# Late blocks' query features from unstacked pairs, in quarters of the PE array's rows, in one run with a chunk's sums

## The chip, the cores and the metric

The kernel runs on one core of one Trainium2 chip. The metric is the device time of one execution in microseconds (us), and a measured time is the median of several executions. The core has a matrix engine (TensorE, "PE" in the profile, with its weight loads listed apart as "PEld"), three engines that work on elements (VectorE "DVE", ScalarE "ACT", GpSimd "POOL"), and a queue engine (SyncE "SP") that here only issues transfers (DMAs). Every engine works through its own list of instructions in order and waits on semaphores for the others. PE reads operands from the on-chip memory SBUF and writes its results to PSUM, eight banks of 128 partitions x 512 float32.

## What is computed

One decoder layer on `x` of shape (2, 2048, 512): linear attention with 16 heads, then cross attention to 154 context rows, then a mixture of experts, each on a layer norm and added to `x`. The change lies in the linear attention alone:

```
q_proj = _elu1(jnp.einsum('bhnd,hdf->bhnf', q, proj_matrix))     # 32 -> 128 features a head
k_proj = _elu1(jnp.einsum('bhnd,hdf->bhnf', k, proj_matrix))
kv = jnp.einsum('bhnf,bhnd->bhfd', k_proj, v)
attn = jnp.einsum('bhnf,bhfd->bhnd', q_proj, kv)
k_sum = k_proj.sum(axis=2)
z = 1.0 / (jnp.einsum('bhnf,bhf->bhn', q_proj, k_sum) + 1e-08)
```

`_elu1(x)` is `x + 1` above zero and `exp(x)` below. Every head has 32 dimensions, so the product that makes its features contracts over 32 rows only.

## The kernel before

The 4096 tokens are eight blocks of 512 (`nblk` = 8, `TB` = 512); four blocks make one batch (`bpb` = 4). Blocks 0 to 3 are called early here, blocks 4 to 7 late. A block's 512 channels are four chunks of 128, and a chunk is four heads. Products that must keep float32 accuracy are made of pairs: a value is split into a high part in the fast format `float32r` and a low part, and three products (high x high, low x high, high x low; the list `TERMS`) are summed in PSUM.

The work on PE is of two kinds. *Dense* work is a queue of generators (`Dense`), each yielding after one matmul; `dense.fill(n)` issues n of them, and `dense.after(n, f)` calls f after n further ones. *Column* work (`columns.matmul`, L229) is pinned to program order with `tc.keep_in_program_order`; the rest may be moved by the scheduler of the tile framework, which writes the final list of each engine from its own timeline. So the order that runs is not the order of the source.

Query features, before. Each chunk of queries lies in DRAM as a pair `qd[b][c]` (high, low; 128 rows x 512 tokens). `load_queries` (L472) reads it with `stack` (L292) in three transfers of 256 KB (high, low, high) into a tile `qst` of 96 partitions: for each head the three parts stand below one another. The projection weights stand likewise stacked in `pst` (high, high, low). One matmul of 96 rows a head (`query_features`, L476, PE line L479, PSUM tile `pqp`) then makes the sum of the three terms at once. `features` (L361) follows: `relu(-x)` on ACT (L364), `exp(-.)` on ACT (L365), and `max(x, 0) + e` on DVE (L366), which is the last reader of the PSUM bank. The banks of `pqp` come from the pool `sc`, which has four.

A chunk's sums: `numerators` (L485, tile `pn`) and `denominators` (L507, tile `pd`) are eight float32 matmuls with 32 columns each, four heads side by side in the array's column quarters, all at L230. Float32 takes two passes, so the trace shows 16 instructions for a chunk.

`attended` (L558) multiplies numerators and reciprocals: POOL (L563, needs the transfers `num<-numd` for early blocks and `zr<-zd`), then ACT (L564), then DVE (L118); the result feeds the output projection `attention_outs` (dense, tile `po_a`, with a load `xr_a`, a POOL add L312 and a DVE add L315).

The late loop (L1346 to L1385) is where the change lies. Its step n handles late chunk n of 16: it loads the next chunk's queries, makes chunk n's features (two heads in each half of the step), fills in 26 (later 28) dense matmuls, calls `attended` for one half block according to the table `ahead` (L1345), and ends with the sums of chunk n - 1. Ahead of it the loop at L1334 ends the keys of the last block; behind it the cross attention begins, whose scores (`psc`) use the same four banks of `sc`.

Of the kernel before, what the change touches and what calls it, by code (L numbers as in the profile page):

```python
# [9 lines left out]
F32 = mybir.dt.float32  # L10
FR = mybir.dt.float32r
# [6 lines left out]
P = 128  # L18
D = 512
NC = D // P  # L20
H = 16
HD = 32
FEAT = 128
TB = 512
# [13 lines left out]
def decoder_layer(  # L38
# [26 lines left out]
    nc = tc.nc  # L65
    tokens = x.shape[0]
    nblk = tokens // TB
    bpb = nblk // batches
# [7 lines left out]
    sc = ctx.enter_context(tc.tile_pool(name="sc", bufs=SC, space=PSUM))  # L76
    dram = ctx.enter_context(tc.tile_pool(name="dram", bufs=1, space=DRAM))
    summed_up = ctx.enter_context(ExitStack())
    rows = ctx.enter_context(ExitStack())
# [18 lines left out]
    def eight(shape, dtype, name):  # L98
        return big.tile(shape, dtype, tag="b8", name=name)

    def half(name, dtype=F32):
        return work.tile([P, 512], dtype, tag="kp", name=name, bufs=9)
# [13 lines left out]
    def low(dst, src, hi, eng=None):  # L116

        (eng or nc.vector).tensor_tensor(dst, src, hi.bitcast(F32), ALU.subtract)  # L118

    def load_weight(w, name):  # L120
        raw = eight([P, NC, w.shape[1]], F32, f"raw_{name}")
        for k in range(NC):
            nc.sync.dma_start(out=raw[:, k], in_=w[k * P : (k + 1) * P, :])
        return [raw[:, k] for k in range(NC)]

    def split_weight(raw, name, busy=False):

        hi = eight([P, NC, D], FR, f"{name}_hi")
        lo = eight([P, NC, D], FR, f"{name}_lo")
        for k in range(NC):  # L130
            if isinstance(raw, list):
                part = raw[k]
            else:
                part = load_tile(raw, 0, k, name)
            if busy:
                nc.gpsimd.tensor_scalar(hi[:, k], part, 1.0, None, ALU.mult)
            else:
                nc.scalar.copy(hi[:, k], part)
            low(lo[:, k], part, hi[:, k], nc.gpsimd if busy or k % 2 else nc.vector)
        return hi, lo  # L140

    TERMS = ((0, 0), (1, 0), (0, 1))
# [90 lines left out]
    columns = Columns()  # L233
# [97 lines left out]
    raw = wk  # L331
    wk = [eight([P, NC, D], FR, f"wk_{i}") for i in ("hi", "lo")]
    for t in range(NT):
# [5 lines left out]
        b = nc.vector.tensor_tensor(lo, pt, hi.bitcast(F32), ALU.subtract)  # L339
        c = nc.scalar.copy(wk[0][:, t], raw[t])  # L340
        d = (nc.gpsimd if t % 2 else nc.vector).tensor_tensor(wk[1][:, t], raw[t], wk[0][:, t].bitcast(F32), ALU.subtract)
# [6 lines left out]
    rest = slice(2 * HD, 3 * HD)  # L348
    low(pst[rest], praw[rest], pst[rest])
    wq = split_weight(load_weight(w_qkv[:, :D], "wq"), "wq")  # L350

    kvs, kszs, pkvs, kaccs, made_kv = [], [], [], [], []
    qd = [[dram.tile([2, P, TB], F32, name=f"qd{b}_{c}") for c in range(NC)] for b in range(nblk)]
# [7 lines left out]
    def features(src, name, e=None):  # L361

        e = half(f"e_{name}") if e is None else e
        nc.scalar.activation(e, src, AF.Relu, scale=-1.0)  # L364
        nc.scalar.activation(e, e, AF.Exp, scale=-1.0)  # L365
        nc.vector.scalar_tensor_tensor(e, src, 0.0, e, ALU.max, ALU.add)  # L366
        return e
# [101 lines left out]

    qsts, qps, pds, nums, numd, zrs, zds, ats = {}, {}, {}, {}, {}, {}, {}, {}  # L470

    def load_queries(b, c):  # L472
        qsts[b, c] = eight([3 * HD, 4, TB], FR, f"qst{b}_{c}")
        stack(qsts[b, c], qd[b][c])

    def query_features(b, c, h):  # L476
        head = slice((4 * c + h) * FEAT, (4 * c + h + 1) * FEAT)
        pp = sc.tile([P, TB], F32, tag="sc", name=f"pqp{b}_{c}_{h}")
        nc.tensor.matmul(pp, lhsT=pst[:, head], rhs=qsts[b, c][:, h, :], start=True, stop=True)  # L479
        e = None  # L480
        if b < bpb and h:
            e = early.tile([P, TB], F32, tag="eq", name=f"eq{b}_{c}_{h}")
        qps[b, c, h] = features(pp, f"q{b}_{c}_{h}", e)

    def numerators(b, c):  # L485
        if c == 0:
# [20 lines left out]
    def denominators(b, c):  # L507
        if c == 0:
            pds[b] = bank(f"pd{b}")
        for h in range(4):  # L510
            columns.matmul(
                pds[b][h * HD : (h + 1) * HD, :],
                lhsT=kszs[b // bpb][:, c, h, :],
                rhs=qps.pop((b, c, h)),
                start=c == 0,
                stop=c == NC - 1,
                skip_group_check=True,
            )
        if c == NC - 1:
            reciprocals(b, pds.pop(b))  # L520
# [23 lines left out]
    def load_numerators(b):  # L544
        nums[b] = eight([P, NC, TB], F32, f"num{b}")
        nc.gpsimd.dma_start(out=nums[b], in_=numd[b])
# [220 lines left out]
    for s in range(ws_gate.shape[1] // F):  # L767
# [9 lines left out]
        out=before,  # L777
        in_=before,
# [503 lines left out]
    chunks = [(b, c) for b in range(nblk) for c in range(NC)]  # L1282
    shift = 2
    per = NC * NT
# [21 lines left out]
    for n in range(nblk * per):  # L1306
        b, c, t = n // per, n // NT % NC, n % NT
        dense.fill(58 if n == 0 else fl(n, 9.25) if n < 32 else fl(n, 9.5))
        if (b, c, t) == (nblk - 1, 0, 0):
            context_load()  # L1310
        if (b, c, t) == (nblk - 1, 1, 0):
            xwk = split_weight(wk_t, "xwk")
            dense.add(*(context_key(i, xwk) for i in range(NC)))
        if (b, c, t) == (nblk - 1, 2, 0):
            xwv = split_weight(wv_t, "xwv")
            bvr = half("bvr")
            nc.sync.dma_start(out=bvr, in_=bv.to_broadcast([P, D]))
            for bt in range(batches):
                dense.add(*(context_value(bt, at, xwv, bvr) for at in range(0, keys, P)))
        if (b, c, t) == (nblk - 1, 3, 0):  # L1320
            load_numerators(0)
            load_reciprocals(0, 0)
            bout = load_row(b_out, "bout")
        dense.until(stks, (b, c))
        key_features(b, c, t)
        todo.append((b, c, t))
        m = n - bpb * per - shift
        if m == -4:
            load_queries(0, 0)
        if m >= 0:  # L1330
            query_step(m)
        if n % 2 and len(todo) > LAG:
            sums_step(m)
    for m in range((nblk - bpb) * per - shift, (nblk - bpb) * per + NT):  # L1334
        dense.fill(5)
        query_step(m)
        if m % 2:
            sums_step(m)
        if m % 4 == 1:
            load_queries(*chunks[bpb * NC])  # L1340

    wout = split_weight(w_out, "wout")
    steps = chunks[bpb * NC :]

    ahead = {n if n < 13 else n + 2: ((n - 1) // 2, (n - 1) % 2 * 2) for n in range(1, 15)}  # L1345
    for n in range(len(steps) + 1):  # L1346
        if n < len(steps):
            b, c = steps[n]
            if n + 1 < len(steps):
                load_queries(*steps[n + 1])  # L1350
        if n + 1 in ahead:
            load_reciprocals(*ahead[n + 1])
        if n == 7:
            ln, tr = layernorm(x1[0], 0, 0, qts, "x")
            dense.add(*ln[:3])
            ln = ln[3:]
        if n == 8:
            dense.add(*tr[:1], *ln, *tr[1:])
        if n == 11:
            dense.add(*(cross_query(0, i) for i in range(NC)))  # L1360
        for i in range(2):
            if n < len(steps):
                query_features(b, c, 2 * i)
                query_features(b, c, 2 * i + 1)
            dense.fill(fl(2 * n + i, 13 if n < 12 else 14))
            if n in ahead:
                attended(ahead[n][0], ahead[n][1] + i)
                if ahead[n][1] and i:
                    whole = ahead[n][0]
                    if whole < nblk - 2:  # L1370
                        dense.add(*attention_outs(whole))
                    if whole + 1 < bpb:
                        load_numerators(whole + 1)
            if n and i:
                columns.batch()
                numerators(*steps[n - 1])
                denominators(*steps[n - 1])
        if n == 10:
            xwq = split_weight(wq_t, "xwq")
        if n == 11:  # L1380
            open_early.clear()
            attending.close()
            res = attending.enter_context(tc.tile_pool(name="res", bufs=1))
            for i in range(NC):
                load_keys(0, i)  # L1385
# [3 lines left out]
    steps = [(b, c, t) for b in range(nblk) for c in range(NC) for t in range(NT)]  # L1389
    for n in range(len(steps) + LAG + 1):  # L1390
        if n < len(steps):
            b, c, t = steps[n]
# [44 lines left out]
        if n > LAG:  # L1437
            b, c, t = steps[n - LAG - 1]
# [47 lines left out]
    for n, (group, u) in enumerate(todo3):  # L1486
# [3 lines left out]
        ahead = [[], []]  # L1490
        if u == len(units) - 2 and more:
            ahead = [expert_ahead(b) for b in range(group[-1] + 1, group[-1] + 3)]
# [8 lines left out]
        if n == LAST:  # L1501
            f0, f1 = finished(g, 0), finished(g, 1)
            d = downs
# [115 lines left out]
```

## Time and profile before

| | |
|---|---|
| median of 3 executions | 2331.12 us (2327.53 to 2331.25) |
| the profiled execution | 2329.48 us, of which the span is 2327.8 us |
| granted PE clock over the span | 0.982 of full speed |
| PE / DVE / ACT / POOL busy | 96% / 72% / 47% / 53% |
| late loop, first to last `pn` and `pd` of late blocks | about 494 to 648 us of the span |
| 486 to 648 us: PE busy, DMA share | 149.59 of 162 us, 0.94 at 260 GB/s |
| stacked query loads `qst<-qd` | 96 transfers of 256 KB in all, 48 of them for late blocks |

How to read it: the span is the time between the first and the last instruction that the profiler saw, and the execution's own time is 1.7 us longer. A matmul's listed duration covers its passage through a pipeline, so matmuls that follow one another overlap and their pace is read from the distance of two starts. A number in brackets behind an instruction is the engine's idle time ahead of it, with what ended it. The DMA share is the mean busy share of 16 DMA engines; values around 1 mean that transfers queue.

### The profile page before, as it was taken

To read this page: it belongs to the slowest core of one execution; us is meant where nothing else is said; L and a number is where in the kernel's file an instruction comes from. 1 tells how busy PE (TensorE), PEld (TensorE's weight loads), DVE (VectorE), ACT (ScalarE), POOL (GpSimd) and SP (SyncE) were. 2 spreads that over 40 slices of the span, in tenths; PEclk is the share of its full clock that TensorE was granted. 3 is DMA by queue.
4 is the path that set the end of the run, shared out by engine and by line. 5 is a ranking of instruction groups with operands and counts; after the bars stand their busy time and mean duration, and the time that the engine had idled before them with its cause. 6 is when DMAs were issued, how large, how long until landed. Compare 5 with 4: busy or idle time off the path is not lost.

```text
span 2327.8 us, 35169 instructions
## 1 busy us (share of the span) xinstructions
PE 2243.1 (96%) x11978; PEld 1740.2 (75%) x11978; DVE 1677.8 (72%) x2733; ACT 1102.0 (47%) x2598; POOL 1224.0 (53%) x1078
## 2 busy tenths in 40 slices
PE   7999999898999999999999999999989999999998
PEld 5888777645667777766788777888878888788887
DVE  6554555568687777778877777787797877877776
ACT  4555776756566777765343343222433223332221
POOL 5545433546475565654765553555484554755543
PEclk9999999999999999999999999999999999999999
DMA  6556777899975566565866657665557656575553
GB/s 211 178 170 179 203 217 217 241 256 268 261 215 149 166 186 167 175 195 212 291 237 228 234 192 295 225 229 217 181 197 293 242 211 231 178 280 208 205 192 129
DMA packets 201809, 498.23 MB, mean 214 GB/s; under 512 B 27738, under 2 KB 47578, under 8 KB 181694
## 3 DMA queue, kind: packets, MB, share of 16 engines
q1 hardware_dynamic: 199902, 489.89, 64.2%
q0 software_dynamic: 1728, 6.09, 0.9%
q8 instruction: 96, 1.57, 0.3%
q14 instruction: 83, 0.68, 0.1%
HBM read 351.30 MB, written 144.60 MB: 213 GB/s over the span
## 4 chain that ended last, share of the span: by engine, by line
PE 73%; DMA 12%; DVE 7%; issue 3%; POOL 2%; ACT 2%; SPq 1%; DVEq 0%; ACTq 0%; POOLq 0%
PE pg L1082 29%; PE pf L1195 11%; PE pf L148 4%; PE pk L148 3%; PE pq L148 3%; PE pv L148 3%; PE po_x L148 3%; PE xpq L148 2%; PE pp L402 2%; PE pc L745 2%; DMA qst<-qd 2%; PE psc L693 2%; PE pkv L230 1%; PE xpt L725 1%; PE po_a L148 1%
## 5 line engine op out<-in xcount | busy, mean ns | idle before, releaser
L1082 PE MATMUL pg<-xo,wq 128*128 128x512 f32 x3360 | 825.2, 392 | 2.5 <-DMA wq<-wqs 1.3
L1082 PEld LDWEIGHTS pg<-xo,wq 128*128 128x128 f32 x3360 | 630.5, 188 | 142.4 <-ACT s L1093 2.0
L1216 DVE TENSOR_TENSOR sum<-sum,pf 128x512 f32<-128x512 f32 x376 | 251.0, 683 | 50.5 <-PE pf L1195 43.9
L407 POOL TENSOR_TENSOR kacc<-kacc,e_k 128x512 f32<-128x512 f32 x128 | 166.1, 1298 | 224.1 <-DVE e_k L366 211.0
L703 ACT ACTIVATE xe<-psc,nb 128x154 f32<-128x154 f32 x512 | 195.2, 414 | 88.2 <-DVE nb L700 84.1
L708 POOL TENSOR_TENSOR xe<-xe,sm 128x616 f32<-128x616 f32 x128 | 157.6, 1237 | 94.5 <-DVE sm L707 73.2
L1195 PE MATMUL pf<-ht,wdo 128*128 128x512 f32 x696 | 188.4, 395 | 10.9 <-DVE sum L1216 10.9
L1145 POOL TENSOR_TENSOR u<-u,gr 128x512 f32<-128x512 f32 x48 | 65.7, 1368 | 238.8 <-DVE u L1114 237.4
L366 DVE SCALAR_TENSOR_TENSOR e_k<-pp,e_k 128x512 f32<-128x512 f32 x128 | 87.4, 685 | 107.5 <-ACT e_k L365 101.7
L1195 PEld LDWEIGHTS pf<-ht,wdo 128*128 128x128 f32 x696 | 130.9, 189 | 41.4 <-DVE sum L1216 12.0
L1195 PE MATMUL pf<-hb,wdo 128*128 128x512 f32 x522 | 148.2, 399 | 0.0
L1113 ACT ACTIVATE u<-u 128x512 f32<-128x512 f32 x80 | 50.6, 633 | 203.1 <-DVE u L1102 202.9
L148 PE MATMUL pf<-wd,hp 128*128 128x512 f32 x528 | 134.9, 403 | 4.7 <-DVE mv_n L248 3.4
L148 PEld LDWEIGHTS pf<-wd,hp 128*128 128x128 f32 x528 | 100.4, 192 | 33.2 <-issue 6.3
L700 DVE TENSOR_REDUCE nb<-psc 128x2 f32<-128x308 f32 x256 | 111.7, 466 | 11.9 <-PE psc L693 11.8
L703 ACT ACTIVATION_READ_ACCUMULATOR xe<-psc,nb 128x1 f32 x512 | 117.2, 229 | 0.0
L1102 DVE TENSOR_TENSOR u<-u,pg 128x512 f32<-128x512 f32 x160 | 108.5, 682 | 10.8 <-PE pg L1082 9.6
L1195 PEld LDWEIGHTS pf<-hb,wdo 128*128 128x128 f32 x522 | 98.1, 189 | 22.4 <-DVE sum L1216 0.8
L364 ACT ACTIVATE e_k<-pp 128x512 f32<-128x512 f32 x128 | 76.8, 601 | 69.7 <-PE pp L402 61.8
L693 PE MATMUL psc<-xkst,xst 96*128 96x154 f32 x512 | 93.8, 291 | 9.2 <-ACT xe L703 8.7
L693 PEld LDWEIGHTS psc<-xkst,xst 96*128 96x128 f32 x512 | 79.7, 197 | 25.2 <-ACT xe L703 16.1
L402 PEld LDWEIGHTS pp<-pst,kst 96*128 96x128 f32 x512 | 75.8, 191 | 26.7 <-issue 8.1
(285 smaller groups left out, 5137.6 us busy)
## 6 DMA issues: line engine op xcount, KB each, us to landing
wq<-wqs SPq DMA_DIRECT2D x90, 1024.0 KB
wqs<-wq SPq DMA_DIRECT2D x30, 1024.0 KB
wdo<-wds SPq DMA_DIRECT2D x29, 1024.0 KB
kst<-kd SPq DMA_DIRECT2D x96, 256.0 KB
qst<-qd SPq DMA_DIRECT2D x96, 256.0 KB
xst<-xqd SPq DMA_DIRECT2D x96, 256.0 KB
wdo<-wds SPq DMA_DIRECT2D x29, 768.0 KB
kd<-khl SPq DMA_DIRECT2D x32, 512.0 KB
```

What stands on the lines that cost most here:

```text
L148: nc.tensor.matmul(dst, lhsT=a, rhs=b, start=n == 0, stop=n == len(todo) - 1)
L366: nc.vector.scalar_tensor_tensor(e, src, 0.0, e, ALU.max, ALU.add)
L402: nc.tensor.matmul(pp[:, h], lhsT=stks[b, c][:, h, rows], rhs=pst[:, head], start=True, stop=True)
L407: nc.gpsimd.tensor_tensor(acc, acc, kp, ALU.add)
L693: nc.tensor.matmul(psc[:, i], lhsT=xsts[b, c][:, h, t * P : (t + 1) * P], rhs=ksts[bt, c][:, h, :], start=True, stop=True,)
L700: nc.vector.tensor_reduce(nb[:, two], psc, AX.X, ALU.max, negate=True)
L703: nc.scalar.activation(e[:, h, :], psc[:, i], AF.Exp, bias=nb[:, h : h + 1], accum_out=sm[:, h : h + 1],)
L708: nc.gpsimd.tensor_tensor(e, e, sm.unsqueeze(2).to_broadcast([P, 4, keys]), ALU.mult)
L1082: nc.tensor.matmul(pb, lhsT=w[:, p, i, k, :], rhs=xop[:, q, k, :], start=first and m == 0, stop=m == len(todo) - 1, skip_group_check=True,)
L1102: nc.vector.tensor_tensor(dst, dst, pb, ALU.add)
L1195: nc.tensor.matmul(banks[i], lhsT=w[:, p, i * P : (i + 1) * P], rhs=t[q], start=new and m == 0, stop=m == len(TERMS) - 1, skip_group_check ...
L1216: nc.vector.tensor_tensor(dst, dst, banks[i], ALU.add)
```

## The change

Late blocks no longer use stacked operands. `load_rows` reads the projection weights once more as plain rows, a head's 32 rows in each quarter of the 128 partitions, and splits them into a pair `prows`. `load_pair` reads two chunks' queries as they lie, high and low, in two transfers of 512 KB into one tile `qh`. `chunk_features` makes a chunk's features of all four heads: for each of the three terms one matmul a head, which contracts over the head's own 32 partitions, so that the four heads stand in the four row quarters of the array; 12 matmuls a chunk in place of 4, into the four banks of `sc`, head 3 first. They are column work, pinned in one order with the sums, and are issued at the end of step n for chunk n + 1, behind the sums of chunk n - 1. The table `ahead` moves the two half blocks of block 5 one step later. Early blocks keep the stacked form.

```diff
+    def load_rows():
+
+        raw = half("prow").rearrange("p (c f) -> p c f", c=NC)
+        for h in range(4):
+            nc.sync.dma_start(
+                out=raw[h * HD : (h + 1) * HD],
+                in_=proj.rearrange("d (c h f) -> d h c f", c=NC, h=4)[:, h],
+            )
+        pair = eight([P, 2, NC, FEAT], FR, "prows")
+        nc.scalar.copy(pair[:, 0], raw)
+        low(pair[:, 1], raw, pair[:, 0], nc.gpsimd)
+        prows.append(pair)
...
+    def load_pair(b, c):
+
+        two = eight([P, 2, 2, TB], FR, f"qh{b}_{c}")
+        for i in range(2):
+            qsts[b, c + i] = two[:, i]
+            nc.sync.dma_start(
+                out=two[:, i].bitcast(F32), in_=qd[b][c + i].rearrange("r p n -> p r n")
+            )
...
+    def chunk_features(b, c):
+
+        pps = [sc.tile([P, TB], F32, tag="sc", name=f"pqp{b}_{c}_{h}") for h in range(4)]
+        for n, (i, j) in enumerate(TERMS):
+            for h in (3, 2, 1, 0):
+                rows = slice(h * HD, (h + 1) * HD)
+                columns.matmul(
+                    pps[h],
+                    lhsT=prows[0][rows, i, c, :],
+                    rhs=qsts[b, c][rows, j, :],
+                    start=n == 0,
+                    stop=n == 2,
+                    skip_group_check=True,
+                )
+        for h in range(4):
+            qps[b, c, h] = features(pps[h], f"q{b}_{c}_{h}")
...
         if (b, c, t) == (nblk - 1, 3, 0):
+            load_rows()
...
-        if m % 4 == 1:
-            load_queries(*chunks[bpb * NC])
+        if m % 4 == 2 and m < (nblk - bpb) * per:
+            load_pair(bpb, 0)
+        if m % 4 == 3 and m >= (nblk - bpb) * per:
+            load_pair(bpb, 2)
+            chunk_features(bpb, 0)
...
-    ahead = {n if n < 13 else n + 2: ((n - 1) // 2, (n - 1) % 2 * 2) for n in range(1, 15)}
+    ahead = {n if n < 11 else n + 1 if n < 13 else n + 2: ((n - 1) // 2, (n - 1) % 2 * 2) for n in range(1, 15)}
...
-            if n + 1 < len(steps):
-                load_queries(*steps[n + 1])
+            if n % 2 and n + 3 < len(steps):
+                load_pair(*steps[n + 3])
...
-            if n < len(steps):
-                query_features(b, c, 2 * i)
-                query_features(b, c, 2 * i + 1)
...
-            if n and i:
+            if i and n:
                 columns.batch()
                 numerators(*steps[n - 1])
                 denominators(*steps[n - 1])
+            if i and n + 1 < len(steps):
+                chunk_features(*steps[n + 1])
```

More of the change, by code (lines that the diff above doesn't have):

```diff
@@ L350, in decoder_layer @@
     wq = split_weight(load_weight(w_qkv[:, :D], "wq"), "wq")
+    prows = []
+    def load_rows():
[9 more added lines that the diff above has]
+        prows.append(pair)
     kvs, kszs, pkvs, kaccs, made_kv = [], [], [], [], []
```

## The prediction

> **What bounds the kernel now.** I read the busy shares first, then a table of the stretch that the change touches, then PE's timeline, its waits, and the engines that those waits lead to.
>
> The page's busy line:
>
> ```profile
> PE 2243.1 (96%) x11978; PEld 1740.2 (75%) x11978; DVE 1677.8 (72%) x2733; ACT 1102.0 (47%) x2598; POOL 1224.0 (53%) x1078
> ```
>
> The late loop by stretches (columns: length, then busy time and count of PE, PEld, DVE, ACT and POOL, then PE clock, DMA share, GB/s):
>
> ```profile
> 493.50:505.80 12.30, 10.64 (x58) 3.61 (x54) 9.38 (x17) 11.07 (x22) 6.71 (x6) 1.00 0.68 193
> 505.80:536.00 30.20, 26.10 (x130) 16.79 (x126) 17.98 (x26) 14.02 (x27) 13.14 (x10) 1.00 1.02 270
> 536.00:648.00 112.00, 105.34 (x519) 65.40 (x520) 83.05 (x128) 66.03 (x127) 64.15 (x61) 0.95 0.94 262
> ```
>
> PE's waits between 493 and 648 us (sum, times, longest):
>
> ```profile
> PE pqp L479 <- DVE e_q L366: 6.9, 6, 2.9
> PE pn L230 <- DVE e_q L366: 1.9, 1, 1.9
> ```
>
> PE bounds the kernel, and the transfers are nearly full in this stretch. PE waits in it mostly for a PSUM bank that DVE gives back when a feature is done. PE's timeline shows the pace, the price of a change of tile shape, and the longest wait:
>
> ```profile
> 514.30 0.39 PE L148 MATMUL po_a<-wout_lo,at 128*128 128x512 f32 x1
> 514.53 0.39 PE L148 MATMUL po_a<-wout_hi,at 128*128 128x512 f32 x1
> 514.85 1.06 PE L230 MATMUL pn<-e_q,kv 128*32 128x512 f32 x8
> 515.73 1.04 PE L230 MATMUL pd<-e_q,ksz 128*32 128x512 f32 x8
> 516.70 0.50 PE L148 MATMUL po_a<-wout_hi,at 128*128 128x512 f32 x1
> 517.04 0.48 PE L479 MATMUL pqp<-qst,pst 96*128 96x512 f32 x1
> ...
> 532.08 1.07 PE L230 MATMUL pn<-e_q,kv 128*32 128x512 f32 x8
> 536.00 0.50 PE L479 MATMUL pqp<-qst,pst 96*128 96x512 f32 x1 [2.86 <-DVE e_q L366]
> ```
>
> A dense matmul takes 0.23 us (514.30 to 514.53), and a stacked `pqp` costs the same slot. Eight column matmuls take 0.88 us (514.85 to 515.73), although each passes for about 0.6: four run side by side. The visit to the 32-column shape costs 0.09 us at its entry (0.32 in place of 0.23), 0.09 at its end (0.97 for 0.88) and 0.11 at the next matmul (0.34): 0.29 in all, 0.145 a change of shape.
>
> The cause of the wait at 536.00 is on POOL and ACT:
>
> ```profile
> 519.02 0.59 POOL L546 DMA_DIRECT2D num<-numd  x1
> 522.55 1.28 POOL L312 TENSOR_TENSOR xr_a<-xr_a,bout 128x512 f32<-128x512 f32 x1 [2.94 <-DVE at L118]
> 530.60 5.87 POOL L563 TENSOR_TENSOR num<-num,zr 128x512 f32<-128x512 f32 x4 [6.77 <-DMA num<-numd]
> ...
> 531.92 0.62 ACT L564 CAST at<-num 128x512 fp32r<-128x512 f32 x1 [6.79 <-POOL num L563]
> ```
>
> Block 2's numerators (1 MB) are asked for at 519.0 and land at 530.6; ACT stands in its queue before the `at` copy, the features behind it are late, and PE waits for their bank. After such waits PE's clock is halved for a while: 0.95 over the 112 us behind 536 means 11 us at half clock, three stretches of some 3.4.
>
> **The change, part by part.** (a) *Streaming.* 64 stacked matmuls of 0.233 us, 14.9 us, go. 192 quarter matmuls come. If four run side by side as the column ones do, a chunk is three rounds; a round of one `float32r` pass I take as one matmul's slot: 48 x 0.233 = 11.2 us. But the changed kernel's instruction list breaks seven chunks' first rounds: 17 quarter matmuls stand alone among dense ones, 17 x 0.233 = 4.0 us. Sum 15.2, so +0.3. Bounds: -3.7 if the lone ones overlap too, and +29.8 if nothing overlaps (192 x 0.233 - 14.9). I take the first, because the nearest row (`pn`, quarters of columns) does overlap.
>
> The Trainium skill, "TensorE: Matmul & The Clock Gate", Part 3, has four row quarters at 3.07 times one matmul's pace, not 4; by it a round would be 0.30 us and this part 3.4 us dearer. No row of this trace has row quarters.
>
> (b) *Changes of shape.* Counted in the two instruction lists from the last key sums to the end of the late loop, PE changes between whole array, column quarters and row quarters 44 times before and 88 times after: a chunk's row run stands with its sums, but adds an edge, and every lone matmul adds two. 44 x 0.145 = 6.4 us. Bounds: 0 (the 96-row `pqp` among dense matmuls shows no price) and 9.0, if each of 33 entries into a row run also exposes the longer weight load (188 against 106 ns, +0.08). I take 0.145: a quarter run is nearer to `pn` than to a 96-row matmul.
>
> The skill's "TensorEngine Tiling (Array Packing)", Key Properties, speaks against this change: a change of tiling mode drains the array. The 0.29 us visit agrees; by the rule the 6.4 stands, without it the row bound 0 would.
>
> (c) *The first steps.* All four banks are now asked for at once, and ACT's list has four relus, then four exps: the last bank comes free 4 x 0.591 + 4 x 0.634 + 0.68 = 5.6 us after a run (rows L364, L365, L366). In full steps that hides behind 26 dense matmuls and the sums (6.1 + 2.0 us) with about 2 us to spare. Until the first output projections there is no dense work: behind chunk 4_0 stand 12 `xpv` (2.8 us), behind 4_1 only sums (2.0), so PE waits 2.8 + 3.6 us; the trace of before has 0.8 + 0.5 there. That is +5.1.
>
> (d) *The copies in ACT's list.* Block 2's `at` copies stood behind the features of 5_0; now they stand between the relus and exps of 4_3. What is queued behind them: those exps, the DVE ops, the run 5_0 and every dense matmul behind it. From the landing of the numerators to the bank: 1.3 + 0.62 + 2 x 0.63 + 0.62 + 2 x 0.63 + 0.68 = 5.7 us, so with the old landing PE goes on at 536.3, as before, but by its list with 48 dense matmuls behind the sums of 4_1, not 74, three groups of sums fewer (3 x 0.88 + one visit) and the features of two chunks fewer: 6.1 + 2.9 + 1.9 = 10.9 us behind. This swallows (c) and the changes of shape up to there. Against it, transfers shrink: late queries are 16 x 512 KB in place of 16 x 768 KB, 4.2 MB less, 0.26 MB more for the weight rows. At 258 GB/s (56.79 MB in 440 to 660 us) that is 15 us of a nearly full DMA. Of the 5 MB between 499 and 531 one goes, 3.9 us. So (c) and (d) together lie between +5 (only c) and +11; with the landing 3.9 earlier, 7; I take +6, as a shorter queue may also speed the first numerators.
>
> (e) *Behind that,* 36 of the 44 added changes of shape remain: +5.2. Waits of before from 536 us on are 0.41, 1.22, 1.02, 0.30, 1.74 and 1.85; the last two end a chain of reciprocal transfers (`zr<-zd`), and cost a half-clock stretch of 3.4 us (1.7 lost) each. The thinner DMA and block 5's later turn should end one of them with its clock loss and most of the other: -5. Bounds: -10 (all with both clock losses) and +5 (another block's copies block like block 2's).
>
> (f) *At nothing:* `load_rows` is four transfers, one copy of 0.6 us on ACT and 1.3 us on POOL, ahead of the first use by two steps; SP issues 28 fewer transfers of about 0.43 us. SP had waits for data at most places, so I count no gain; without the cover the four row transfers could cost some 2 us once. At the loop's end chunk 7_3's run is followed by only its neighbour's sums and 6 dense matmuls (3.4 us) against 5.6: a wait of 2.2, where 1.85 is now.
>
> Sum: 0.3 + 6 + 5.2 - 5 = +6.5 on 2329.48 is 2336.0; the median lies 1.6 above the profiled execution, so 2337.
>
> **The rivals.** *Faster, because the transfers give.* Place: the waits behind `num<-numd` and `zr<-zd`. If they end (2.86 + 1.74 + 1.85 + 0.52 for a late `qst`, and three half-clock losses of 1.7: -12.1) and the changes of shape cost half (+3.2), the time is 2322. It decides once the numerators of block 2 land 6 us earlier. For it speaks the DMA share of 1.02; against it that ACT's list now asks for them earlier. *No difference:* PE's additions fall into waits that stay, since transfers set the pace: 2331. The share of 0.94 speaks for it, 105 of 112 busy us on PE against. *The quarters do not overlap:* +29.8 and the shape changes, 2365; nothing in the trace but the missing rows speaks for it.
>
> **How the numbers follow.** Mine 0.50, faster 0.22, no difference 0.18, no overlap 0.10. The measurement can tell about 0.2%, 4.7 us. Of mine, 0.06 falls within that: faster 0.22, same 0.24, slower 0.54. The range leaves out no overlap and the far ends: from 2321 (the faster rival) to 2352 (mine with the upper bounds of b and d, 2.6 + 5, and 7 of the 10 between the value and the bound of e). Mine alone is 2333 to 2347.
>
> **What would show it.** Quarter matmuls of one round start together, and 12 take about 0.7 us; the matmul behind a row run starts 0.1 late; PE waits of 2 to 4 us ahead of the runs 4_1 and 4_2; a wait ahead of 5_0 ended by DVE, with ACT's `at` behind POOL behind `num<-numd`; DMA moves about 4 MB less. I am wrong if the visits cost nothing, if the numerators land well ahead of 525 us, or if each quarter matmul takes its own slot.

## The result and the profile after

The changed kernel takes 2371.3 us (median; 2368.28 to 2371.84) beside 2330.03 us for the kernel before (2327.53 to 2331.25): a ratio of 1.0172, 95% interval 1.0157 to 1.0187. The change costs 41 us. The forecast had the sign and not the size: 2337, with a range up to 2352.

Where the time lies is found by setting the matmuls of the two traces beside each other by their place in PE's list. From the last key work ahead of the late loop to a matmul of the cross attention some 70 us behind the loop's last sums, the same stretch of work is 474.4 to 715.6 us before and 471.5 to 752.5 us after: 241.2 and 281.0 us. Behind it the changed kernel loses another 4 us, and ahead of the stretch it gains 3. The loop's last sums (`pd`) start at 643.5 and 683.7 us, so the loop holds nearly the whole loss. The table of that stretch, first of the kernel before, then of the changed one (columns: length, then busy time and count of PE, PEld, DVE, ACT and POOL, then PE clock, DMA share, GB/s):

```profile
474.40:715.60 241.20, 222.79 (x1182) 142.87 (x1182) 174.29 (x299) 142.84 (x367) 140.45 (x128) 0.95 0.88 245
```

```profile
471.50:752.50 281.00, 245.75 (x1311) 147.06 (x1314) 172.24 (x303) 140.11 (x371) 139.16 (x129) 0.90 0.66 199
```

DVE, ACT and POOL do the same work as before. PE is idle for 35.25 us (281.00 - 245.75) in place of 18.41: +16.8. Its clock is halved for 54.6 us in place of 23.9 by the granted-clock records; half of the difference, 15.4 us, is the most that this can cost. That leaves 7.6 us at least for the matmuls themselves. And over the whole stretch the transfers are no longer full: a share of 0.66 where it was 0.88.

PE's waits in that stretch of the changed kernel, longest groups (sum, times, longest):

```profile
PE pqp L230 <- DVE e_q L380: 18.8, 8, 7.2
PE po_a L148 <- DVE num L545: 4.5, 2, 2.8
PE psc L733 <- DVE e_q L380: 2.8, 2, 2.3
```

They are the same kind of wait as before (a bank that DVE has not given back), grown from 6.9 to 18.8 us. Two of DVE's own waits, first of the changed kernel, then the second of them in the kernel before:

```profile
DVE at L118 <- ACT at L604: 28.1, 10, 7.1
DVE z L577 <- DMA z<-dd: 15.4, 4, 5.5
```

```profile
DVE z L537 <- DMA z<-dd: 2.7, 3, 1.1
```

The wait for ACT's `at` copies was there before (26.1 us); the one for the reciprocal's transfer grew from 2.7 to 15.4 us, and features stand behind it in DVE's list. Not all of that reaches PE: the longest of these waits, 5.5 us at 594.4, falls in a stretch (586 to 596 us) in which PE is busy all the time.

The first large stall, on PE's timeline of the changed kernel, with a lone quarter matmul further on:

```profile
491.65 0.96 PE L230 MATMUL pqp<-qh,prows 32*128 32x512 f32 x12
492.54 0.64 PE L148 MATMUL xpv<-xwv_hi,ct 128*26 128x512 f32 x2
...
496.87 1.09 PE L230 MATMUL pqp<-qh,prows 32*128 32x512 f32 x2 [1.37 <-DVE e_q L380]
502.65 2.24 PE L230 MATMUL pqp<-qh,prows 32*128 32x512 f32 x10 [4.69 <-DVE e_q L380]
...
508.28 2.78 PE L230 MATMUL pqp<-qh,prows 32*128 32x512 f32 x12 [0.26 <-DVE e_q L380]
510.99 1.93 PE L230 MATMUL pn<-e_q,kv 128*32 128x512 f32 x8
...
517.77 0.39 PE L148 MATMUL po_a<-wout_lo,at 128*128 128x512 f32 x1
518.09 0.50 PE L230 MATMUL pqp<-qh,prows 32*128 32x512 f32 x1
518.52 0.73 PE L148 MATMUL po_a<-wout_hi,at 128*128 128x512 f32 x2
519.09 0.40 PE L148 MATMUL po_a<-wout_lo,at 128*128 128x512 f32 x1
```

Three things are to be read here. When all four banks are free, 12 quarter matmuls take 0.89 us to the next matmul (491.65 to 492.54): the rows do overlap. When they are not, the same 12 take 2.71 us (508.28 to 510.99): the single starts of that run lie 0.60 us apart in the first round, which is the distance at which DVE finishes one feature after another. PE's clock was full in that stretch, so the pace is DVE's, and the waits list does not show it, because a quarter matmul passes for 0.5 us. And a lone quarter matmul costs 0.63 us: 0.32 in place of 0.23 ahead of it, 0.43 for itself, 0.57 in place of 0.46 for the two behind it.

DVE at the same stall, in the changed kernel:

```profile
496.14 1.27 DVE L380 SCALAR_TENSOR_TENSOR e_q<-pqp,e_q 128x512 f32<-128x512 f32 x2
501.49 0.55 DVE L577 RECIPROCAL z<-z 128x64 f32<-128x64 f32 x1 [4.08 <-DMA z<-dd]
501.96 1.22 DVE L380 SCALAR_TENSOR_TENSOR e_q<-pqp,e_q 128x512 f32<-128x512 f32 x2
```

The reciprocal of block 3 now stands between the second and the third feature of chunk 4_0 and waits for a transfer, and the run of 4_1 waits behind it with two of its banks. Before, it stood behind the first feature of 4_1 and waited 0.61 us. The reciprocal itself starts at nearly the same time in both kernels, at 500.57 and 501.49; what differs is what stands behind it.

The last large stall, 7.21 us, has three links. PE, ACT, POOL and the SP queue of the changed kernel:

```profile
661.75 0.50 PE L230 MATMUL pqp<-qh,prows 32*128 32x512 f32 x1
...
670.36 2.84 PE L230 MATMUL pqp<-qh,prows 32*128 32x512 f32 x11 [7.21 <-DVE e_q L380]
```

```profile
656.62 0.65 ACT L379 ACTIVATE e_q<-e_q 128x512 f32<-128x512 f32 x1
665.05 0.62 ACT L604 CAST at<-num 128x512 fp32r<-128x512 f32 x1 [7.78 <-POOL num L603]
665.58 1.66 ACT L379 ACTIVATE e_q<-e_q 128x512 f32<-128x512 f32 x3
```

```profile
663.76 2.48 POOL L603 TENSOR_TENSOR num<-num,zr 128x512 f32<-128x512 f32 x2 [9.62 <-DMA zr<-zd]
```

```profile
647.33 1.71 SPq L591 DMA_DIRECT2D zr<-zd  x4
...
649.61 4.53 SPq L294 DMA_DIRECT2D xst<-xqd  x6
654.18 0.90 SPq L591 DMA_DIRECT2D zr<-zd  x2
655.19 0.38 SPq L300 DMA_DIRECT2D xqd<-xhl  x1
655.62 1.17 SPq L591 DMA_DIRECT2D zr<-zd  x2
```

An `at` copy stands in ACT's list between the first exponential of 7_2 and the other three. It needs POOL's product, POOL needs the second half of block 6's `zr`, and SP issued that behind six stacked loads of the cross attention (4.53 us). So three features are late, PE's run 7_3, which needs their banks, stops after one of its 12 matmuls for 7.21 us, and the clock is halved from 667.9 to 684.9 us. The transfers are full here, whatever the mean of the stretch says: their share (the last column but one) is 1.05 and 1.07 while these parts of `zr` are issued and under way.

```profile
650.00:655.00 5.00, 5.00 (x29) 2.08 (x33) 1.92 (x4) 1.45 (x3) 2.52 (x2) 1.00 1.05 274
655.00:660.00 5.00, 5.00 (x27) 3.64 (x20) 2.40 (x4) 2.27 (x5) 0.00 (x0) 1.00 1.07 222
```

### The profile page after: what moved, and what is told of

Same layout as the page of the kernel before. It is cut to its first block, busy times and chain, and to the rows that moved or that the text cites. A ratio compares the mean times of both kernels' runs of the same rounds, so it can differ in the third digit from the quotient of the medians.

```text
span 2369.1 us, 35365 instructions
## 1 busy us (share of the span) xinstructions
PE 2263.5 (96%) x12106; PEld 1740.9 (73%) x12106; DVE 1673.7 (71%) x2733; ACT 1099.2 (46%) x2599; POOL 1223.5 (52%) x1079
## 4 chain that ended last, share of the span: by engine, by line
PE 52%; DVE 6%; DMA 5%; ACT 2%; POOL 1%; issue 1%; SPq 0%; DVEq 0%; ACTq 0%; POOLq 0%
PE pg L1122 29%; PE pf L1235 11%; PE pf L148 4%; PE po_x L148 2%; DMA xsx<-x 2%; ACT xe L743 1%; PE pc L785 1%; PE psc L733 1%; PE xpt L765 1%; DMA x<-xr_x 1%; DMA xqd<-xhl 1%; PE xpq L148 1%; DVE nb L740 1%; PE ptf L845 1%; PE pto L1274 0%
## 5 line engine op out<-in xcount | busy, mean ns | idle before, releaser
L1235 PE MATMUL pf<-ht,wdo 128*128 128x512 f32 x696 | 189.5, 397 | 10.9 <-DVE sum L1256 10.9
L733 PEld LDWEIGHTS psc<-xkst,xst 96*128 96x128 f32 x512 | 78.5, 196 | 28.0 <-ACT xe L743 17.4
```

Of the source, the lines that this page charges most:

```text
L733: nc.tensor.matmul(psc[:, i], lhsT=xsts[b, c][:, h, t * P : (t + 1) * P], rhs=ksts[bt, c][:, h, :], start=True, stop=True,)
L1235: nc.tensor.matmul(banks[i], lhsT=w[:, p, i * P : (i + 1) * P], rhs=t[q], start=new and m == 0, stop=m == len(TERMS) - 1, skip_group_check ...
```

## The experiments

Theories at the start: RUN, that one run for four heads (four banks asked for at once, four relus and four exponentials in a block) makes the waits; QUARTERS, that the row quarters and their changes of shape cost the time; and, for the waits, ACT-QUEUE, that the `at` copies in ACT's list make them. LOCKSTEP is the form of RUN in which PE and ACT take turns whatever stands in their lists; CHAIN, formed after the first four runs, puts the waits down to the reciprocals' transfers, and PLACE, formed after the first eight, to the place of the instructions that wait for them.

For each kernel the same stretch of work is measured against the kernel before: its length, and of that PE's idle time and half of the added half-clock time; the rest is the difference. Idle time at half clock is in both, so the rest comes out low where waits are long. Each row is one profiled execution. In e1, e2, e5 and e9 the next matmul behind the end of the stretch waits 3.2 to 4.6 us for the cross attention's `cx`, which it does not in the other kernels; these waits are not in the table.

| kernel | median us (ratio to before, 95%) | stretch | idle | clock | rest |
|---|---|---|---|---|---|
| changed | 2371.3 (1.0172; 1.0157 to 1.0187) | +39.8 | +16.8 | +15.4 | +7.6 |
| e1, run alone | 2358.25 (1.0098; 1.0071 to 1.0125) | +25.0 | +23.8 | +5.1 | -3.9 |
| e2, quarters alone | 2356.62 (1.0085; 1.0057 to 1.0113) | +25.3 | +5.7 | +10.2 | +9.4 |
| e3, changed, `at` on POOL | 2376.91 (1.0186; 1.0162 to 1.0211) | +52.4 | +22.2 | +27.3 | +2.9 |
| e4, before, `at` on POOL | 2349.4 (1.006; 1.0038 to 1.0081) | +21.2 | +15.2 | +12.0 | -6.0 |
| e5, changed, heads 0 to 3 | 2365.71 (1.0135; 1.0117 to 1.0153) | +35.2 | +19.0 | +12.0 | +4.2 |
| e6, changed, turns as before | 2377.64 (1.0184; 1.016 to 1.0207) | +39.6 | +18.8 | +16.1 | +4.7 |
| e7, changed, no reciprocals | 2351.43 (1.0073; 1.0052 to 1.0093) | +14.7 | +1.1 | +4.4 | +9.2 |
| e8, before, no reciprocals | 2321.95 (0.9954; 0.9938 to 0.9969) | -5.4 | -0.7 | -3.4 | -1.3 |
| e9, changed, reciprocals later | 2372.06 (1.0176; 1.0157 to 1.0196) | +33.8 | +13.2 | +17.4 | +3.2 |
| e10, e9 and e5 together | 2357.79 (1.0115; 1.0085 to 1.0145) | +24.3 | +5.5 | +10.1 | +8.7 |
| e11, before, reciprocals later | 2334.24 (1.0009; 0.9995 to 1.0024) | +0.4 | +3.4 | -1.7 | -1.3 |

**The run alone.** The changed kernel with the old stacked operands, four matmuls of 96 rows in one pinned run at the same place (loads of `qst` one or two steps ahead, no `load_rows`, no `load_pair`):

```diff
-        for n, (i, j) in enumerate(TERMS):
-            for h in (3, 2, 1, 0):
-                rows = slice(h * HD, (h + 1) * HD)
-                columns.matmul(pps[h], lhsT=prows[0][rows, i, c, :], rhs=qsts[b, c][rows, j, :], ...
+        for h in (3, 2, 1, 0):
+            head = slice((4 * c + h) * FEAT, (4 * c + h + 1) * FEAT)
+            columns.matmul(pps[h], lhsT=pst[:, head], rhs=qsts[b, c][:, h, :], start=True, stop=True)
```

> The changed kernel with its four heads in one pinned run at the same place, last bank first, but with the stacked 96-row operands of before (4 matmuls a chunk, three transfers a chunk, 38 changes of tile shape in PE's list in place of 88). Theory RUN (the loss is the single run on all four banks, which makes PE wait for ACT and DVE and halves PE's clock): still clearly slow, 2350 to 2372 us, waits of PE for DVE's e_q of 12 us or more and 40 us or more at half clock in the late loop. Theory QUARTERS (row quarters and their changes of shape cost the time): back at 2328 to 2340 us.

2358.25 us, 25 more than the kernel before, and almost all of it idle time: +23.8, with no loss in the matmuls. The DMA share in the stretch is 0.79. The time is in RUN's range, but its two signs are not there: the waits for `e_q` are 8.4 us in all, not 12 or more, and 34 us are at half clock, not 40. The longest wait, 10.5 us ahead of `psc` at 669.2, has another cause: in DVE's list the layer norm's `st_x`, which waits for a transfer (`xsx<-x`, 5.4 and 1.5 us), stands ahead of the features of 7_3, which come only from 668.4 on. So most of this idle time is not the wait for four banks itself; the new place of the run lets in other waits.

**The quarters alone.** Pairs and quarter matmuls, but two heads at a time, at the places that the kernel before had, with its table of turns:

```diff
-    def chunk_features(b, c):
+    def chunk_features(b, c, heads):
-            for h in (3, 2, 1, 0):
+            for h in heads[::-1]:
...
+            if n < len(steps):
+                chunk_features(b, c, (2 * i, 2 * i + 1))
-            if i and n + 1 < len(steps):
-                chunk_features(*steps[n + 1])
```

> Pairs and row quarters as in the changed kernel, but the features of a chunk in two halves of two heads, each at the place where before had them (start of each half step), six matmuls at a time; block 5's attended as before. 90 changes of tile shape (before 44: +6.7 us by the visit's price), 96 slots of 0.233 us in place of 64 (+7.5), 3.9 MB less to move. RUN: 2332 to 2350 us, waits for e_q near those of before (7 us). QUARTERS: 2360 us or more.

2356.62 us: between the two expectations, with waits for `e_q` of 8.4 us, near those of before, as RUN said. A run of six quarter matmuls takes 0.89 us to the next matmul where nothing delays it, as long as a run of 12 (three rounds of 0.33, 0.22 and 0.32 us with two heads as with four), and there are nearly twice as many runs. Little idle time is added, but the clock is halved for longer and the matmuls cost 9.4 us.

So neither RUN nor QUARTERS is the cause by itself. Each costs about 25 us in the stretch, by different ways (idle time the one, matmuls and clock the other), and together they cost 40, less than the sum.

**The copies in ACT's list.** The high part of `at` is made by POOL in place of ACT, in the changed kernel and, as a control, in the kernel before:

```diff
-        nc.scalar.copy(ats[b][0][:, c], at)
+        nc.gpsimd.tensor_scalar(ats[b][0][:, c], at, 1.0, None, ALU.mult)
```

> The changed kernel with the copy of attended's product (at, high part) on POOL in place of ACT, so that no feature stands behind it in ACT's list. Theory ACT-QUEUE (features are late because ACT stands before an at copy that waits for POOL and a transfer): 2338 to 2352 us, and the wait for e_q falls from 18.8 us to under 10. Theory LOCKSTEP (one run of four banks is too tight with or without these copies): 2360 us or more.

> The kernel before with the same move of the at copy from ACT to POOL. ACT-QUEUE: the waits of 2.86, 1.74 and 1.85 us and part of their half-clock stretches go, 2318 to 2326 us. LOCKSTEP: nothing of before hangs on it, 2328 to 2334 us; POOL gets 1.3 us more for each of 28 copies, which could cost up to 5 us where the output projection waits for it.

2376.91 and 2349.4 us. ACT-QUEUE falls as a remedy: with the copies gone from ACT's list the wait for `e_q` is 16.9 us, not under 10, PE's idle time grows, and DVE now stands for POOL, in the waits of the changed kernel with this move:

```profile
DVE at L118 <- POOL at L604: 30.1, 8, 13.0
```

The control misses both its ranges: the same move costs 14 us by the ratio in the kernel before, which has 15.2 us more idle time by it (in a profiled execution 6.7 us above the median). POOL gets 44 us more work in the stretch (184.2 in place of 140.5), so the pair does not test the place of the copies alone; ACT-QUEUE is not settled by it.

**The order of the heads.** The changed kernel with head 0 first:

```diff
-            for h in (3, 2, 1, 0):
+            for h in range(4):
```

> The changed kernel with the heads of a round in the order 0, 1, 2, 3 in place of 3, 2, 1, 0; nothing else. In the changed kernel's trace a run often starts with one to three quarter matmuls, and the rest waits some us later. BANK ORDER theory (the order of the heads sets how much of the run's wait comes in the middle of the run and what lone quarters cost): the time moves by 6 us or more against 2371, down to about 2360 if the waits come ahead of the run and the half clock behind them (54.6 us) shrinks. CHAIN theory (the waits are set by what the other engines' in-order lists wait for, whichever head comes first): 2366 to 2376, PE's idle time in the late loop within 4 us of 35.3.

2365.71 us, 5.6 below the changed kernel's median and by the ratios 0.4% (8.6 us), with intervals that just miss each other. The stretch is 4.6 us shorter, by clock and matmuls; the idle time is not less, 37.4 us beside 35.3. So the order of the heads is worth something, as BANK ORDER said, though less than its 2360, and the waits stay, as CHAIN said.

**The turns.** The changed kernel with the table `ahead` of before:

```diff
-    ahead = {n if n < 11 else n + 1 if n < 13 else n + 2: ((n - 1) // 2, (n - 1) % 2 * 2) for n in range(1, 15)}
+    ahead = {n if n < 13 else n + 2: ((n - 1) // 2, (n - 1) % 2 * 2) for n in range(1, 15)}
```

> The changed kernel with the table of turns as it was before the change: block 5's attended tiles come one step earlier. CHAIN theory: the reciprocals of block 5 are asked for earlier than they can be there, one more wait of 3 to 6 us at block 5's turn, 2373 to 2385; or, if the later turn is itself what pushes block 6 behind the stacked loads (the stall of 7.2 us at 663), that stall shrinks and the time is 2358 to 2368. LOCKSTEP theory (PE and ACT take turns over the four banks, whatever the turns): 2366 to 2376.

2377.64 us; the number lies in CHAIN's first range, but the intervals of the two ratios overlap and the stretch is as long as with the later turns, so this part of the change is worth nothing that can be measured, in either direction. The late stall is 8.05 us here, not shorter, so block 5's later turn was not what pushed block 6 behind the stacked loads.

**Without the reciprocals.** Both kernels without the way from the denominators to `zr`: no copy back, no reciprocal, no store, no loads of `zr`; POOL adds the numerators to themselves at the place of the product. The attention is thus not divided by its denominators.

```diff
-        z = small.tile([P, H * TB // P], F32, tag="z", name=f"z{b}", bufs=1)
-        ...
-        dense.after(10, turned)
-        dense.after(26 if b < nblk - 1 else 24, stored)
...
-        nc.gpsimd.tensor_tensor(at, at, zrs.pop((b, c)), ALU.mult)
+        nc.gpsimd.tensor_tensor(at, at, at, ALU.add)
```

> The changed kernel without the reciprocals' chain: the copy back of the denominators, the reciprocal, its store and the 56 loads of zr are left out, and POOL adds the numerators to themselves in place of the product with zr (the same shape). To be read against the same cut of the kernel before. CHAIN theory (most of the loss is waits for z<-dd on DVE and zr on POOL, with the half clock behind them): this kernel falls to 2340 to 2350, and its distance to the kernel before with the same cut is 15 us or less. LOCKSTEP theory (four banks in one run make PE and ACT take turns, and the chain only shows where): the distance stays at 30 us or more. Between 15 and 30 both carry a part.

> The kernel before with the same cut (no copy back of the denominators, no reciprocal, no store of it, no loads of zr; POOL adds the numerators to themselves). Both theories: the kernel before waits little for the chain (2.7 us of DVE, two PE waits of 1.74 and 1.85 with a half-clock stretch each), so 2318 to 2331.

2351.43 and 2321.95 us. By the ratios the chain costs the changed kernel 1.0% (23 us) and the kernel before 0.5% (11 us); the distance between their medians falls from 41 to 29.5, between the two expectations and close to LOCKSTEP's. The changed kernel misses CHAIN's 2340 to 2350 by a little. The table of the stretch, of the changed kernel and of the kernel before, both without the chain:

```profile
474.90:730.80 255.90, 236.42 (x1310) 144.60 (x1306) 174.02 (x296) 138.18 (x366) 129.36 (x129) 0.94 0.57 177
```

```profile
475.00:710.70 235.70, 218.05 (x1180) 142.74 (x1172) 172.15 (x296) 140.34 (x367) 125.89 (x124) 0.96 0.74 209
```

Without the chain the two kernels are idle for nearly the same time, 19.5 and 17.7 us, so what is left of the distance is not LOCKSTEP's waiting. In these two profiles the stretch is 20.1 us longer with the change: 1.8 idle, 7.8 clock, 10.5 matmuls. (The profiled execution without the chain in the changed kernel is 5 us faster than its median, so the stretch shows less than the medians' 29.5.) So in these two profiles the added idle time goes with the reciprocals' chain; the added cost of the matmuls and half of the clock loss do not. The pair leaves out the chain's places in the lists and its traffic together (the share falls to 0.57), so it does not tell which of the two makes the waits.

**The reciprocals later.** In the changed kernel, and in the kernel before as a control, the reciprocals of blocks 3 and 4 are made 34 dense matmuls behind their denominators; a third run (e10) has this move and the order of the heads 0 to 3 together:

```diff
-        dense.after(26 if b < nblk - 1 else 24, stored)
+        dense.after(34 if b in (bpb - 1, bpb) else 26 if b < nblk - 1 else 24, stored)
```

> The changed kernel with the reciprocals of blocks 3 and 4 asked for 34 dense matmuls after their denominators in place of 26. On DVE z3 then stands behind the four features of 4_1, not between the features 1 and 2 of 4_0, and z4 behind those of 5_2. PLACE theory (the stall of 4.69 us at 498 is DVE waiting for z<-dd in the middle of a run's features): that stall shrinks to 1.5 us or less, with the half clock behind it (10.2 us), so 2358 to 2366; chunk 4_1's sums start 3 to 5 us sooner. LOCKSTEP theory (the run waits for its four banks anyway, the reciprocal only ended last): a wait of 3 us or more stays there, 2366 to 2376.

> The changed kernel with both: the reciprocals of blocks 3 and 4 later, as in the run before this one, and the heads in the order 0, 1, 2, 3. PLACE theory: the gains add, 2352 to 2361. LOCKSTEP theory: as with the order of the heads alone (2365.7), 2361 to 2371.

> The kernel before with the reciprocals of blocks 3 and 4 asked for 34 dense matmuls after their denominators: z3 goes from behind the first feature of 4_1 to behind its second, z4 six features later. Both theories: the kernel before waits 2.7 us for z<-dd in all, so 2328 to 2337; PLACE theory has no reason for more than 4 us in either direction.

2372.06, 2357.79 and 2334.24 us. PE's timeline of the changed kernel with the reciprocals later:

```profile
500.39 0.96 PE L230 MATMUL pqp<-qh,prows 32*128 32x512 f32 x12
...
505.61 3.44 PE L230 MATMUL pqp<-qh,prows 32*128 32x512 f32 x12 [1.37 <-DVE e_q L380]
508.98 1.94 PE L230 MATMUL pn<-e_q,kv 128*32 128x512 f32 x8
510.69 1.93 PE L230 MATMUL pd<-e_q,ksz 128*32 128x512 f32 x8
512.55 3.33 PE L230 MATMUL pqp<-qh,prows 32*128 32x512 f32 x12
515.81 1.94 PE L230 MATMUL pn<-e_q,kv 128*32 128x512 f32 x8
```

The wait of 4.69 us is gone, as PLACE said: from the run of 4_0 to the sums of 4_1 it is 15.4 us (500.39 to 515.81) where the changed kernel takes 19.3 (491.65 to 510.99). What stays is a wait of 1.37 us, within PLACE's 1.5 and not LOCKSTEP's 3, and a run that takes 3.4 us because its banks come at DVE's pace and, from 507.1 on, the clock is halved. The stretch is 6.0 us shorter in the profile, yet the time is the same, so PLACE's 2358 to 2366 is missed: this kernel loses 7.7 us ahead of the late loop (a wait of 4.6 us for a key feature with 20.5 us at half clock around and behind it). Whether the move causes that loss the runs do not tell; e10, with the same move, loses 3.9 us there. With both edits the time is 2357.79 us, 13 us below the changed kernel with intervals apart, in PLACE's range, and the idle time is down to 5.5 us over the kernel before. But the interval overlaps that of e5 (the heads' order alone), so what the move adds to it is not clear of the noise. The same move in the kernel before changes nothing. No version here beats the kernel before.

## Why the prediction was off, step by step

The step that failed is (e), the waits that were to end; the clock, charged to no new wait, is the largest omission beside it.

- **(a) and (b), the matmuls, +6.7: right in kind, too low.** The quarters overlap and the shape changes cost, so neither bound that denied one of them held. By the rows, 17 lone quarter matmuls at 0.63 us and 16 runs at 0.09 + 0.89 make 26.4 us where 64 stacked matmuls took 14.9: +11.5. A round costs 0.27 us ((0.89 - 0.09) / 3), not one slot of 0.233, and a lone visit 0.63, not 0.52. The table's rest where waits are short is near it: 8.7 us in e10, 9.4 in e2, 10.5 for e7 over e8. The Trainium skill, "TensorE: Matmul & The Clock Gate", Part 3, gives 3.07 times one matmul's pace for four row quarters; here four in 0.27 us against 0.233 are 3.5 times.
- **(c), the first steps, +5.1: the place right, one cause missed.** The bank is late there for the reason given, but on top of it DVE's own list now has `z3` between two features. With `z3` moved away (e9) 1.37 us of wait and some 1.8 us of DVE's pace are left ahead of 4_1, near the 2.8 predicted. The changed kernel's listed waits for 4_1 and 4_2 (1.37 + 4.69 + 0.26 us) come to the predicted 6.4 only by luck: 4.1 of them are the reciprocal's. The expected form was wrong too: the waits lie inside the run, since head 3's bank was one of those free first.
- **(d), block 2's numerators: the place right, the early landing mostly luck.** They land at 527.0, 3.6 us before the old 530.6 (predicted 3.9, by thinner transfers), but 2.9 of this is that they are asked for earlier (516.1 in place of 519.0); the transfer takes 10.9 us in place of 11.6. `at` copies lie between the exponentials of 4_3, and PE waits 2.10, 0.98 and 0.41 us there. By the sums of chunk 5_1, the first behind the 2.86 us that the kernel before waits at 536.00, the changed kernel is 13.6 us late (558.7 in place of 545.1), though the loop began 1.9 us earlier: 15.5 us where (c) and (d) together were put at +6. The sum left out the wait of `z3` and, for all new waits, the clock.
- **(e), +5.2 of edges and -5 of ended waits: this is the step that failed.** It said that a thinner DMA and block 5's later turn would end the late waits for reciprocals. The DMA did get thinner (3.9 MB less, as counted), and the waits grew: DVE's for `z<-dd` from 2.7 to 15.4 us, and a new PE wait of 7.21 us behind `zr<-zd`; the turn did nothing that can be measured (e6). From the sums of 5_1 to those of 7_3 the changed kernel falls back another 26.2 us, where +0.2 was predicted: 8.2 us of it at chunk 6_2 and 15.8 us at 7_2 and 7_3. At 6_2 PE waits 2.82 and 1.73 us, with 10.2 us at half clock, while ACT and DVE stand before the `at` copies of block 5; POOL makes the products of the first half at 602.0, after 2.10 us of waiting for `zr<-zd`, and those of the second only from 607.9 on, behind two other operations of its own of 1.75 us. At 7_3 it is the 7.21 us, with 17.1 us at half clock. What these waits have in common is the place of an instruction in a list that is worked in order: `z` among DVE's features, `at` among ACT's exponentials, `zr` behind other loads on SP. For `z3` e9 shows it, since the wait goes with the place. For `zr` at 7_3 it is argued: the transfers were full from 650 to 660 us, and no run takes the place apart from them. The prediction reads the list of after for ACT and PE, not for DVE's reciprocals and SP's `zr` loads.
- **The clock.** Two ended waits were credited with their half-clock loss, but no new wait was charged with one. The added half-clock time is 30.7 us, up to 15.4 us of loss: nearly as much as the added idle time. About half of it stays without the reciprocals (e7 over e8, 7.8 us), when the idle time is nearly the same.
- **(f), at nothing: agrees.** No wait for the rows' weights shows; the longest wait at the loop's end is 2.3 us (`psc`), predicted 2.2, with 0.5 and 0.3 beside it.
- **The rivals.** "Faster, because the transfers give" had its condition met in part (the numerators came earlier, the DMA share fell) and still did not come true, for the reason under (e). "No overlap" falls by the 0.89 us, though a run held to DVE's pace looks like it: 2.71 us for 12 is 0.226 each. "No difference" assumed that transfers set a pace into which PE's additions would fall; they did not.

## What to carry to other kernels

Where engines work through lists in order and their slack is small, read the new list of every engine for instructions that wait on a transfer, and ask what stands behind each of them; here a thinner DMA did not shorten these waits. A mean share of transfers over a long stretch hides the places where they are full. Charge each new wait of PE with its clock loss as well as its length. Joining work into one run asks for all of its banks at once, and then the run goes at the pace of the engine that gives the banks back, which a list of waits may not show.

## What was not expected of the hardware

- The half clock came in steps of about 3.4 us, and its length did not follow from the wait alone. In the kernels without quarter matmuls (before, e1, e4) waits of 1.7 to 3.5 us had one or two steps, those of 5.0 and 6.5 us two and one of 7.3 us three. With quarter matmuls there were sometimes more: five at the wait of 7.21 us, and in e2 four (537.1 to 550.7) at one of 2.94 us, with dense matmuls between the quarter runs; but a wait of 7.23 us in e5 had three. With the reciprocals later, a wait of 1.37 us was followed by 13.7 us at half clock (507.1 to 520.8), although no further wait is listed there: the work was row-quarter runs, the first rounds of them at DVE's pace, and 32-column sums, with no dense matmul until 519.4. With both edits 13.7 us again (502.5 to 516.2) followed two waits of 0.50 and 0.69 us, in the same kind of work. That quarter matmuls release the clock late would fit this and the clock loss of e2 and e7, but no run took it apart from the waits, so it is left open. The Trainium skill, "TensorE: Matmul & The Clock Gate", Part 1, has windows of about 3.4 us, of idleness for the halving and of activity for the release; the steps agree, but here waits well below one window were enough.
- A run of quarter matmuls costs three rounds whatever its width: 0.89 us for 6, 9, 11 or 12 of them with free banks.
- What stays open: of the 29.5 us that are left between the two kernels without the reciprocals, the profiles place 20 in the stretch and 4.6 behind it; the other 5 lie between the profiled execution of the changed one and its median. Nor does a run show why the run alone and the quarters alone cost 25 us each and together only 40.
